# First attention of a two-block transformer kernel: statistics of later chunks taken earlier, right sums placed behind the key and value closes, and first roots by two tiles

## The chip, the cores and the metric

The kernel runs on one core of a Trainium2 chip. Its time is the device time of one execution in microseconds (us). Before the change, three executions took 1986.58, 1987.5 and 1990.99 us; the median is 1987.5. The engines are called as in the profile: PE is TensorE, with PEld for its weight loads, DVE is VectorE, ACT is ScalarE, POOL is GpSimd, and SP issues most DMAs.

## The reference

The input x holds 2048 tokens of 512 float32 features; a second sequence of the same size, ctx, supplies keys and values. Four layers follow one another, each on a layernorm of x and each added to x: an attention, a feed-forward layer, a second attention, and a mixture of experts. The change is in the first attention alone:

```python
q = (layernorm(x) @ Wq + bq).reshape(B, L, 8, 4, 128)         # 8 groups of 4 heads
k_, v_ = jnp.split(ctx @ Wkv + bkv, 2, axis=-1)               # 8 key and value heads
attn = softmax(einsum('bkglm,bmkd', scores of q and k) / sqrt(128))
x = x + (einsum('bkglm,bmkd->blkgd', attn, v).reshape(B, L, 4096) @ Wo + bo)
```

Attention runs within a sequence of 64 tokens (there are 32 of them). The layernorm of x needs a mean, a variance and an inverse square root for each token.

## The kernel before, in words

**Tiles and chunks.** The rows of x stay on the chip as 16 tiles of 128 tokens (`xs`); four tiles make a chunk of 512 tokens, and there are four chunks. The first attention is a loop over 32 turns, `order`: chunks 0 and 1 alternate through the eight groups of heads (turns 0 to 15), then chunks 2 and 3 do (turns 16 to 31). A turn computes one group's queries, scores and softmax for one chunk, and finishes the turn before it: turning the attention weights (`pt_o`), mixing the values (`po_o`) and projecting out to x (`ppx_o`, `ppy_o`, `ppz_o`).

**Products by seven quarters.** The large products (queries, keys and values, output) are made from seven products of quarter matrices instead of eight. This needs sums and differences of quarters on both sides: `left_sums` (L436 to L439) and `right_sums` (L446 to L449), four `tensor_tensor` instructions each. The weights' and context's sums run on POOL; those of the queries' right side, made from the normalised rows, run on DVE. A product is finished by a close, a DVE addition of a PSUM bank and a kept part: L641 for queries, L573 for keys and values. A PSUM bank can be used again only when its close has read it. The pool `ps_mm` has four banks and serves `pt_a`, `pz`, `py`, `pw`, `pt_o`, `pqy`, `pqz`, `pqv`, `po_o`, `ppy_o` and `ppz_o` in turn.

**The rows of a chunk.** Before a chunk's first turn, `attn0_in(c)` prepares its rows: `chunk_stats` takes mean and variance of each of the four tiles (L383, L386) and the inverse root of all four at once. Chunks 0 and 1 use `first_inv_sqrt` (two ACT steps, L368 and L369, then one Newton step), chunks 2 and 3 use `inv_sqrt` (three Newton steps on DVE, L353 to L362). DVE then writes a normalised tile h (L496), PE transposes it in four pieces (`pt_a`, L502), ACT copies it out of PSUM into `rows_q` (L507), and DVE makes the right sums. Chunk 1 is prepared after turn 0, chunk 2 after turn 15, chunk 3 after turn 16. At the end of each turn but the last few, `make_kv` makes keys or values for a later turn; it comes in the code after `attn0_in`. For chunks 2 and 3, `add_bias` adds the output bias to the rows of x on POOL (L486) once the rows h have been read.

**What sets the order.** A planner orders the instructions of each engine by its own costs. `pin` keeps an instruction in program order against other pinned ones of its engine. All of PE's matmuls in this stage are pinned; on DVE the query closes are pinned, and the statistics of chunks 2 and 3 (L383); on POOL the sums before turn 1 are pinned through the class `InOrder`. [...]

Of the kernel before, what the change touches and what calls it, by code (L numbers as in the profile page):

```python
# [12 lines left out]
ALU = mybir.AluOpType  # L13
# [9 lines left out]
TT = CH // P  # L23
# [6 lines left out]
def layers(ctx: ExitStack, tc: tile.TileContext, a: dict, out: bass.AP):  # L30
    nc = tc.nc
# [67 lines left out]
    def pin(ins):  # L99
        return tc.keep_in_program_order(ins)  # L100
# [92 lines left out]
    xs = [X[:, i, :] for i in range(NC * TT)]  # L193
# [218 lines left out]
    def chunk_stats(c, name, **how):  # L412
        return row_stats(xs[c * TT : (c + 1) * TT], name, **how)
# [28 lines left out]
    def right_sums(engine, b11, b12, b21, b22, sums, t3=None):  # L442

        t1, t2, t4 = (sums[:, i] for i in range(3))
        t3 = b12 if t3 is None else t3
        engine.tensor_tensor(t1, b12, b11, ALU.subtract)  # L446
        engine.tensor_tensor(t2, b22, t1, ALU.subtract)
        engine.tensor_tensor(t3, b22, b12, ALU.subtract)
        engine.tensor_tensor(t4, b21, t2, ALU.subtract)  # L449
        return {"11": b11, "21": b21, "22": b22, "1": t1, "2": t2, "3": t3, "4": t4}  # L450
# [25 lines left out]
    class InOrder:  # L476


        def tensor_tensor(self, *operands):
            pin(nc.gpsimd.tensor_tensor(*operands))  # L480

    adder = [InOrder()]

    def add_bias(c):
        for x in xs[c * TT : (c + 1) * TT]:
            adder[0].tensor_tensor(x, x, bo, ALU.add)  # L486

    def attn0_in(c):

        hx = rows_q[c % 2]  # L490
        roots = first_inv_sqrt, inv_sqrt
        mv, rstd = chunk_stats(c, f"a{c}", root=roots[c // 2], pinned=c > 1)
        for t in range(TT):
            x = xs[c * TT + t]
            h = t2(f"h_a{c}_{t}")
            nc.vector.tensor_scalar(  # L496
                h, x, mv[:, t, 0:1], rstd[:, t : t + 1], ALU.subtract, ALU.mult
            )
            pt = ps_mm(f"pt_a{c}_{t}")
            for k in range(KT):  # L500
                pin(
                    nc.tensor.transpose(  # L502
                        pt[:, k * P : (k + 1) * P], h[:, k * P : (k + 1) * P], ident
                    )
                )

            nc.scalar.copy(  # L507
                hx[:, t // 2 : t // 2 + 3 : 2, :, (t % 2) * P : (t % 2) * P + P],
                pt.rearrange("p (i k n) -> p i k n", i=2, k=2),
            )  # L510
        return right_sums(nc.vector, hx[:, 0], hx[:, 1], hx[:, 2], hx[:, 3], hx[:, 4:7])

# [20 lines left out]
    def ctx_right(c):  # L535
        x = ctx_q[c % 2]
        return right_sums(adder[0], x[:, 0], x[:, 1], x[:, 2], x[:, 3], ctx_sums[c % 2])

    def attn0_kv(value, g, c, left, right):
        n = f"{'kv'[value]}{g}_{c}"  # L540
        for i in range(2):
            kv[value, g + i, c] = kv_free.pop(0)
        dst = [kv_tiles[:, kv[value, g + i, c], :] for i in range(2)]

        def product(ps, x, y, first=True):
            x, y = left[x], right[y]
            for m in range(2 if value else 1):
                for k in range(2):
                    sides = (y[:, k, m * P : (m + 1) * P], x[:, k, :]) if value else (
                        x[:, k, :], y[:, k, :]  # L550
                    )
                    out_ps = ps[:, m * P : (m + 1) * P] if value else ps[:, 0:256]
                    pin(
                        nc.tensor.matmul(  # L554
                            out_ps, *sides, start=first and m == k == 0, stop=k == 1,
                            skip_group_check=True,
                        )
                    )

        kept = [t2(f"u_{n}_{i}") for i in range(2)]  # L560

        def keep(ps, i, at):
            u = kept[at // 2][:, at % 2 * 256 : at % 2 * 256 + 256]
            if value:
                nc.scalar.copy(u, ps[:, 0:256])
            else:
                nc.scalar.activation(
                    u, ps[:, 0:256], AF.Identity, bias=bkv[:, g + i : g + i + 1]
                )
            return u  # L570

        def close(i, half, ps, u):
            nc.vector.tensor_tensor(  # L573
                dst[i][:, half * 256 : half * 256 + 256], ps[:, 0:256], u, ALU.add
            )

        x = ps_tr(f"px_{n}")
        product(x, "11", "11")
        u1 = keep(x, 0, 0)
        z = ps_mm(f"pz_{n}")  # L580
        product(z, "1", "1")
        z1 = keep(z, 1, 1)
        y = ps_mm(f"py_{n}")
        product(y, "12", "21")
        close(0, 0, y, u1)
        product(x, "2", "2", first=False)
        u2 = keep(x, 0, 2)
        product(z, "4", "22", first=False)
        close(0, 1, z, u2)
        y = ps_mm(f"pw_{n}")  # L590
        product(y, "22", "4")
        product(x, "3", "3", first=False)
        u3 = keep(x, 1, 3)
        close(1, 1, x, z1)
        close(1, 0, y, u3)

# [161 lines left out]
    order = [(2 * i + j, g) for i in range(NC // 2) for g in range(NG) for j in range(2)]  # L758
# [8 lines left out]
    def kv_chunk(p, j):  # L767

        return 2 * (2 * p // NG) + j, 2 * p % NG

    def make_kv(value, p, j):
        c, g = kv_chunk(p, j)
        attn0_kv(value, g, c, kv_lefts[value], ctx_rights[c])

    rights = {0: attn0_in(0)}
    attn0_first_keys(0, 0, w_k)
    open_visit(0)
    kv_lefts = [kv_left(w_k, 0), None]
# [7 lines left out]
    for i in range(len(order) + 1):  # L786
        q = iter(())
        if i < len(order):
            c, g = order[i]
            visit = visits[i // 2]  # L790
            q = attn0_queries(g, c, visit["q"], rights[c])
        if last is not None:
            gl, cl, atl = last
            atT = attn0_turn(gl, cl, atl)
        next(q, None), next(q, None)
        if last is not None:
            o = attn0_out(gl, cl, attn0_mix(gl, cl, atT), visits[(i - 1) // 2]["o"])
        else:
            o = iter(())
        for _ in range(3):  # L800
            next(q, None)
        for _ in range(2):
            next(o, None)
            qT = next(q, None)
        next(o, None), next(o, None)
        if i < len(order):
            at = attn0_scores(g, c, qT)
            last = (g, c, at)
        else:
            fold_latent(latent)  # L810
        for _ in range(3):
            next(o, None)
        if i == len(order):
            break
        if i % 2 == 0:
            if i > 0:
                visit["o"] = right_sums(nc.gpsimd, *w_quarters(visit["w"][1]), wo_sums)
            if i // 2 + 1 < len(visits):
                w_next = load_attn0(order[i + 2][1], (i // 2 + 1) % 2)
        else:  # L820
            if i // 2 + 1 < len(visits):
                open_visit(i // 2 + 1)
            else:
                nc.sync.dma_start(gamma, a["gamma"].broadcast_to([P, HID]))
                nc.sync.dma_start(beta, a["beta"].broadcast_to([P, HID]))
                up, latent = load_up()
                ups = []
                for j in range(2):
                    k11, k12, k21, k22 = w_quarters(up[:, :, j * 512 : (j + 1) * 512])
                    ups.append(left_sums(nc.gpsimd, k11, k21, k12, k22, up_sums[j]))  # L830
            if i % 4 == 1:
                clear_list(i // 4)
        if i + 1 < len(order):
            cn, gn = order[i + 1]
            if cn not in rights:
                rights[cn] = attn0_in(cn)
                if cn > 1:
                    add_bias(cn)

        p, step = divmod(i, 4)  # L840
        if i == 0:
            add_bias(1)
            adder[0] = nc.gpsimd
            make_kv(0, 0, 1)
        if step < 2:
            make_kv(1, p, step)
        elif p + 1 < NP:
            make_kv(0, p + 1, step - 2)
        cp, gp = kv_chunk(p, step % 2)
        if step < 2 and gp == NG - 2 and cp + 2 < NC:  # L850
            load_ctx(cp + 2, ctx_q[cp % 2])
            ctx_rights[cp + 2] = ctx_right(cp + 2)
        if step == 0 and p + 1 < NP:
            kv_lefts[0] = kv_left(load_kv(kv_chunk(p + 1, 0)[1], 0), 0)
        elif step == 1 and p + 1 < NP:
            kv_lefts[1] = kv_left(load_kv(kv_chunk(p + 1, 0)[1], 1), 1)
# [164 lines left out]
    for c in range(NC):  # L1021
# [6 lines left out]
        else:  # L1028
            load_ctx(2, ctxT[2])
            mv, rstd = chunk_stats(0, "b0", rms=True)  # L1030
# [537 lines left out]
    for i in range(NI + 1):  # L1568
        c, b = divmod(i, 8)
# [161 lines left out]
```

## Time and profile before

| | |
|---|---|
| median of the runs | 1987.5 us |
| profiled execution | 1988.88 us |
| its span, first to last instruction | 1987.0 us |
| mean granted PE clock | 0.982 |
| PE, DVE, ACT, POOL busy | 95%, 53%, 26%, 28% of the span |
| first attention | from the start to about 1220 us |

A busy share is an average over the whole kernel; what a stage costs is read from that stage. Three views matter here. The windows view gives the busy time of each engine in a stretch, with the clock that the throttle granted to PE (1.00 is full speed). The chain of work that ended last, in order of time, names at each step the piece of work that set the end; where an engine other than PE stands in it, PE was waiting for that work. The timeline gives single instructions, and in brackets how long an engine was idle before one and what ended this.

### The profile page before, as it was taken

How to read it: one execution, taken by the hardware profiler on the slowest of the kernel's cores; microseconds unless marked ns; L12 is line 12 of the kernel's file. 1: busy time of each engine (PE TensorE's matmuls, PEld its weight loads, DVE VectorE, ACT ScalarE, POOL GpSimd, SP SyncE). 2: the span in 40 equal slices, each digit the busy share in tenths (PEclk: the TensorE clock that was granted, in tenths of full speed). 3: DMA queues.
4: the chain of work that ended last, by engine and by line, in shares of the span. 5: the costliest groups of instructions: out<-in, count | busy, mean ns of one | idle time of the engine just before them, and what ended most of it. 6: DMA issues, size and time to landing. Idle time of an engine off the chain costs nothing.

```text
span 1987.0 us, 26632 instructions
## 1 busy us (share of the span) xinstructions
PE 1888.4 (95%) x10544; PEld 1545.4 (78%) x10544; DVE 1056.9 (53%) x2077; ACT 519.9 (26%) x1019; POOL 548.3 (28%) x581
## 2 busy tenths in 40 slices
PE   7999999999998799999999999999999999879993
PEld 5888988889887698998998987787777776655441
DVE  6455445445546754454454456455466466663415
ACT  2211212212212222122122122311221565543221
POOL 7221121121322211211211211141344535540115
PEclk9999999999999899999999999999999999989997
DMA  9992110111210101111110012000004201214628
GB/s 330 307 301 89 39 43 33 33 43 40 67 43 11 43 33 32 43 32 33 43 32 22 22 59 88 19 1 11 0 22 138 64 12 54 85 71 133 217 94 271
DMA packets 129882, 151.72 MB, mean 76 GB/s; under 512 B 4704, under 2 KB 84384, under 8 KB 129760
## 3 DMA queue, kind: packets, MB, share of 16 engines
q1 hardware_dynamic: 118752, 122.70, 19.5%
q0 software_dynamic: 5392, 17.11, 2.6%
q10 hardware_dynamic: 5616, 10.23, 1.4%
q8 instruction: 84, 1.38, 0.3%
q14 instruction: 38, 0.31, 0.1%
HBM read 92.60 MB, written 56.36 MB: 75 GB/s over the span
## 4 chain that ended last, share of the span: by engine, by line
PE 88%; DVE 6%; DMA 2%; ACT 2%; issue 1%; POOL 1%; POOLq 0%; SPq 0%; DVEq 0%; ACTq 0%
PE ppx_o L464 11%; PE pqx_a L464 9%; PE sc_a L106 6%; PE pqz_a L464 6%; PE ppz_o L464 6%; PE py L106 6%; PE po_o L106 3%; PE pp L106 3%; PE pdx_f L464 3%; PE pqv_a L464 3%; PE ppy_o L464 3%; PE pqy_a L464 3%; PE px_v L554 2%; PE phx_f L464 2%; PE px_k L554 2%; PE pq_b L106 2%
## 5 line engine op out<-in xcount | busy, mean ns | idle before, releaser
L405 ACT ACTIVATE at_a<-at_a 128x512 f32<-128x512 f32 x64 | 40.4, 631 | 444.0 <-DVE at_a L404 444.0
L106 PE MATMUL py<-arena,xT 128*128 x312 | 140.8, 593 | 0.4 <-ACT xT L1447 0.2
L633 ACT ACTIVATE u_a<-pqx_a,bq 128x256 f32<-128x256 f32 x192 | 80.6, 471 | 163.4 <-PE pqx_a L464 161.1
L464 PE MATMUL ppx_o<-weights,oT_o 128*128 128x256 f32 x512 | 122.8, 383 | 0.1
L464 PE MATMUL pqz_a<-arena 128*128 128x256 f32 x512 | 121.0, 379 | 0.0
L464 PE MATMUL pqx_a<-arena,weights 128*128 128x256 f32 x512 | 121.0, 379 | 0.0
L106 PEld LDWEIGHTS sc_a<-kv,qT_a 128*128 128x128 f32 x1024 | 119.4, 192 | 1.7
L106 PE MATMUL sc_a<-kv,qT_a 128*128 128x64 f32 x1024 | 117.9, 273 | 0.0
L729 DVE TENSOR_TENSOR x<-ppx_o,x 128x512 f32<-128x512 f32 x128 | 86.9, 679 | 46.5 <-PE ppx_o L464 44.6
L464 PEld LDWEIGHTS pqz_a<-arena 128*128 128x128 f32 x512 | 97.2, 190 | 13.6 <-issue 0.4
L641 DVE TENSOR_TENSOR qT_a<-pqz_a,u_a 128x512 f32<-128x512 f32 x64 | 44.3, 692 | 113.9 <-ACT u_a L633 81.1
L464 PEld LDWEIGHTS pqx_a<-arena,weights 128*128 128x128 f32 x512 | 94.9, 190 | 12.0 <-DMA arena<-in_ctxT 0.2
L464 PEld LDWEIGHTS ppx_o<-weights,oT_o 128*128 128x128 f32 x512 | 94.8, 190 | 12.0 <-ACT oT_o L719 0.5
L106 PEld LDWEIGHTS py<-arena,xT 128*128 128x128 f32 x312 | 56.1, 190 | 56.5 <-issue 56.0
L446 POOL TENSOR_TENSOR arena<-weights 128x512 f32<-128x512 f32 x15 | 19.1, 1272 | 270.3 <-PE ppz_o L464 270.3
L436 POOL TENSOR_TENSOR arena<-weights 128x512 f32<-128x512 f32 x17 | 21.8, 1286 | 204.0 <-PE pqz_a L464 200.9
L436 POOL TENSOR_TENSOR kv_room<-weights 128x256 f32<-128x256 f32 x14 | 10.7, 762 | 238.6 <-DMA weights<-in_Wkv 238.6
L641 DVE TENSOR_TENSOR qT_a<-pqy_a,u_a 128x512 f32<-128x512 f32 x32 | 22.1, 692 | 101.5 <-PE pqy_a L464 101.5
L1466 DVE TENSOR_TENSOR y<-py,weights 128x512 f32<-128x512 f32 x39 | 26.9, 691 | 85.0 <-PE py L106 77.2
L403 DVE TENSOR_REDUCE mx_a<-sc_a 128x8 f32<-128x512 f32 x64 | 44.3, 692 | 44.3 <-PE sc_a L106 44.3
L106 PE MATMUL po_o<-atT_o,kv 64*128 64x256 f32 x512 | 65.9, 392 | 0.8 <-ACT atT_o L698 0.8
L1015 POOL TENSOR_TENSOR s_f<-s_f,arena 128x512 f32<-128x512 f32 x16 | 21.5, 1361 | 157.0 <-DVE s_f L1012 117.1
(427 smaller groups left out, 4264.9 us busy)
## 6 DMA issues: line engine op xcount, KB each, us to landing
xg<-zero SPq DMA_DIRECT2D x8, 4096.0 KB, 20.1
weights<-in_Wq SPq DMA_DIRECT2D x16, 1024.0 KB, 5.3
weights<-in_Wo SPq DMA_DIRECT2D x16, 1024.0 KB, 5.3
xr<-xg SPq DMA_DIRECT2D x39, 256.0 KB, 3.5
yg<-y ACTq DMA_DIRECT2D x39, 256.0 KB, 2.2
weights<-in_Wkv SPq DMA_DIRECT2D x16, 512.0 KB, 3.4
arena<-in_W_e SPq DMA_DIRECT2D x8, 1024.0 KB, 6.1
x<-in_x SPq DMA_DIRECT2D x16, 256.0 KB, 8.3
```

What stands on the lines that cost most here:

```text
L106: nc.tensor.matmul(ps, lhsT, rhs, start=(i == 0), stop=(i == len(pairs) - 1))
L403: nc.vector.tensor_reduce(mx, p3, AX.X, ALU.max)
L405: nc.scalar.activation(dst, dst, AF.Exp, scale=scale)
L436: engine.tensor_tensor(s1, a21, a22, ALU.add)
L446: engine.tensor_tensor(t1, b12, b11, ALU.subtract)
L464: nc.tensor.matmul(ps[:, m, :], left[:, k, m * P : (m + 1) * P], right[:, k, :], start=first and m == i == k == 0, stop=i == len(pairs) - ...
L554: nc.tensor.matmul(out_ps, *sides, start=first and m == k == 0, stop=k == 1, skip_group_check=True,)
L633: nc.scalar.activation(u[:, m * 256 : (m + 1) * 256], ps[:, m * 256 : (m + 1) * 256], AF.Identity, bias=bq[:, 4 * g + 2 * heads + m : 4 * ...
L641: nc.vector.tensor_tensor(q5[:, heads, :, 4 * half : 4 * half + 4, :], ps.rearrange("p (m b q) -> p m b q", m=2, q=64), u.rearrange("p (m ...
L729: nc.vector.tensor_tensor(dst, ps.rearrange("p (m n) -> p m n", m=2), dst, ALU.add)
L1015: nc.gpsimd.tensor_tensor(y, y, gamma, ALU.mult)
L1466: pin(nc.vector.tensor_tensor(y, py, be1[:, bass.ds(v[1], 1), :], ALU.add))
```

## The change

There are three parts. Each is in the first attention, and none changes what is computed.

The statistics and roots of chunks 2 and 3 are taken after turns 4 and 8, between that turn's output and its value product, and kept until the chunk's rows are made. The rows themselves are still asked for after turns 15 and 16.

`attn0_in` now returns the transposed rows only. Their right sums are a function of their own, `attn0_right`; for chunks 1, 2 and 3 it is called behind `make_kv`, and both its sums and the closes of keys and values are pinned in program order on DVE.

Chunks 0 and 1 take their roots by two tiles at a time instead of by four, still with `first_inv_sqrt`.

```diff
     class InOrder:
+        def __init__(self, engine):
+            self.engine = engine
+
         def tensor_tensor(self, *operands):
-            pin(nc.gpsimd.tensor_tensor(*operands))
-
-    adder = [InOrder()]
+            pin(self.engine.tensor_tensor(*operands))
+
+    adder = [InOrder(nc.gpsimd)]
...
-    def attn0_in(c):
+    def attn0_in(c, stats=None):
         hx = rows_q[c % 2]
-        roots = first_inv_sqrt, inv_sqrt
-        mv, rstd = chunk_stats(c, f"a{c}", root=roots[c // 2], pinned=c > 1)
+        if stats is None:
+            stats = []
+            for i in range(0, TT, 2):
+                mv, rstd = row_stats(
+                    xs[c * TT + i : c * TT + i + 2], f"a{c}_{i}", root=first_inv_sqrt
+                )
+                stats += [(mv[:, j, 0:1], rstd[:, j : j + 1]) for j in range(2)]
+        else:
+            mv, rstd = stats
+            stats = [(mv[:, j, 0:1], rstd[:, j : j + 1]) for j in range(TT)]
         for t in range(TT):
             x = xs[c * TT + t]
             h = t2(f"h_a{c}_{t}")
-            nc.vector.tensor_scalar(
-                h, x, mv[:, t, 0:1], rstd[:, t : t + 1], ALU.subtract, ALU.mult
-            )
+            nc.vector.tensor_scalar(h, x, *stats[t], ALU.subtract, ALU.mult)
...
-        return right_sums(nc.vector, hx[:, 0], hx[:, 1], hx[:, 2], hx[:, 3], hx[:, 4:7])
+        return hx
+
+    def attn0_right(hx, engine):
+        return right_sums(engine, hx[:, 0], hx[:, 1], hx[:, 2], hx[:, 3], hx[:, 4:7])
...
+    ordered = InOrder(nc.vector)
...
         def close(i, half, ps, u):
-            nc.vector.tensor_tensor(
+            ordered.tensor_tensor(
                 dst[i][:, half * 256 : half * 256 + 256], ps[:, 0:256], u, ALU.add
             )
...
-    rights = {0: attn0_in(0)}
+    rights, stats = {0: attn0_right(attn0_in(0), nc.vector)}, {}
...
             cn, gn = order[i + 1]
+            if i in (4, 8):
+                stats[i // 4 + 1] = chunk_stats(i // 4 + 1, f"a{i // 4 + 1}", pinned=True)
             if cn not in rights:
-                rights[cn] = attn0_in(cn)
+                hx = attn0_in(cn, stats.get(cn))
                 if cn > 1:
                     add_bias(cn)
...
             make_kv(0, p + 1, step - 2)
+        if i + 1 < len(order) and cn not in rights:
+            rights[cn] = attn0_right(hx, ordered)
```

## The prediction

> **What bounds the kernel now.** First the page's busy line and its chain by engine:
>
> ```profile
> PE 1888.4 (95%) x10544; PEld 1545.4 (78%) x10544; DVE 1056.9 (53%) x2077; ACT 519.9 (26%) x1019; POOL 548.3 (28%) x581
> ...
> PE 88%; DVE 6%; DMA 2%; ACT 2%; issue 1%; POOL 1%; POOLq 0%; SPq 0%; DVEq 0%; ACTq 0%
> ```
>
> TensorE carries the chain; VectorE is busy half the time, so its work costs only where TensorE waits for it. The windows view (span; then busy time and count of PE, PEld, DVE, ACT, POOL; granted clock, DMA share, GB/s) says where that is in the first attention:
>
> ```profile
> 78.00:560.00 482.00, 482.00 (x2760) 430.94 (x2760) 245.16 (x405) 102.55 (x208) 95.78 (x86) 1.00 0.28 85
> ...
> 604.00:624.00 20.00, 13.59 (x63) 11.75 (x64) 13.12 (x32) 5.54 (x11) 5.54 (x4) 0.83 0.08 27
> ...
> 656.00:678.00 22.00, 15.47 (x104) 14.07 (x105) 18.29 (x66) 5.75 (x12) 5.56 (x4) 0.77 0.00 1
> 678.00:1200.00 522.00, 522.00 (x2967) 465.73 (x2964) 266.23 (x440) 111.83 (x226) 95.66 (x84) 1.00 0.11 35
> ```
>
> Two stretches have no pause at all. Between them lie two pauses, one after turn 15 and one after turn 16, where the granted clock falls too. The chain (start, duration, what) says what TensorE waits for there, and shows two more places, at 10 and at 50 us:
>
> ```profile
> 7.43 0.70 DVE st_a L383
> ...
> 9.65 0.56 DVE h_a L496
> ...
> 48.39 1.67 DVE arena L449
> 50.06 0.34 DVE kv L573
> ...
> 603.29 0.69 DVE x L729
> 603.98 0.61 DVE st_a L383
> ...
> 609.40 3.83 DVE h_a L496 x4
> 613.37 1.08 PE pt_a L502 x4
> ```
>
> Each is VectorE preparing query rows: statistics (L383), root, normalised rows (L496), or the right sums (L446 to L449) ahead of the key and value closes (L573).
>
> **The two pauses.** I price them by turn length, which takes in the slow matmuls after a pause:
>
> ```profile
> 557.65 3.52 PE sc_a L106 x32
> 594.50 3.52 PE sc_a L106 x32
> ...
> 643.10 3.52 PE sc_a L106 x32
> 694.96 3.52 PE sc_a L106 x32
> 732.02 3.52 PE sc_a L106 x32
> ```
>
> From scores to scores a turn with a key product takes 36.85 (557.65 to 594.50), one with a value product 37.06 (694.96 to 732.02). The two in question take 48.60 and 51.86. Each must keep its 16 transposes: 16 times 0.109 us, from eight pt_o transposes in 0.87, makes 1.74. Without a pause they would take 38.59 and 38.80: gains of 10.0 and 13.1.
>
> Are the pauses really free of cover? In the built order of the changed program the statistics of chunks 2 and 3 leave this place for turns 4 and 8, and VectorE issues the four rows h_a inside turns 15 and 16: two behind the left sums, one behind the close of pqv, one behind the last query close. There VectorE idled 2.77 us (before L641 at 585.05) and 1.04 twice. A row costs 0.48 (1.92 for four, alone) to 1.3 (2.60 for two beside POOL): the first two need 2.6 at most and fit; the others may be 0.3 late, on closes that TensorE needs about 3 us later (pqv closes at 587.63; scores start at 594.34). So nothing; with that cover gone, 1.9 to 5.2 us a turn. The transposes then need four PSUM banks; the last is freed by the ppz add that ends at 602.40, before TensorE arrives at 603.27. The first attention's clean case is turn 0, where pt_a follows the scores at once and the key product follows 1.59 us later, never waiting for ACT's four 0.59 us copies.
>
> What slides into the emptied place is the FFN's statistics of chunks 0 and 1: four of L383 and their roots, 20 instructions, now before and between the first closes. Laid out from 602.5 with 0.6 us per statistic and 0.2 per dependent small step, the first close comes at about 607.9 (TensorE's py_k ends 607.7) and the second at 609.8. The first to wait for that second close is pt_o's second bank, at 603.27 + 1.74 + 6.06 (seven products of 0.866) + 0.44 = 611.5. Covered by 1.7 us. The four right sums, pinned behind the last close, take 2.7 (four L446 to L449 from 669.91 to 672.53) in a hole of 3.24 (idle before L641 at 677.35). Zero, with 0.5 to spare; the next in VectorE's queue is the query close of pqy, and po_o's second pair of banks waits for it. The bias adds on POOL (L486, 5.5 us) move ahead with the rows; in turn 15 three stand before L439, where POOL idled 4.86, and that sum isn't read for 20 us. SP's order and its DMAs don't change.
>
> **Turns 4 and 8.** Their statistics and roots (20 instructions, 603.90 to 609.36 in the trace, 5.46 us) are pinned between the last output add and the first value close. In turn 4 that add ends at 197.45, so the first close starts at 202.85 in place of 199.51, and the second, 0.34 behind it with 0.42 to run, ends at 203.62. The second pt_o bank waits for that, and was due at 203.25: 0.4 us lost, twice, -0.8. Ends: 0, and 2.5 if POOL slows every small step (one L361 took 1.23 beside POOL at 665.26); POOL has only L449 there, and L383 ran at its usual 0.69 beside POOL at 17.52, so I take 0.8.
>
> **The start.** The fourth tile's statistics start when its DMA lands, at 7.43, before and after. Then came mean, variance, two ACT steps, three Newton steps: first row at 9.65. By two tiles, the first pair's variance and ACT steps (0.2 each) run while VectorE waits for tiles three and four; three Newton steps of 0.2 are left behind 8.14, so the first row comes at 8.74. The second pair's steps slip between rows, and TensorE needs 0.91 per tile (3.65 for four), more than VectorE. Gain 0.9; the ceiling is the context. Its last DMA is issued around 5.2, lands 9.0 later at 14.2, and pk's third slice would now come at 14.6. I take 0.85; ends 0 and 0.95.
>
> **Turn 0's end.** Now the right sums of chunk 1 no longer stand before the closes. The second softmax product can start at 42.5 and, at 1.75 beside POOL, ends at 44.3; the closes follow, the second ends about 45.1, and TensorE's py_v starts at 46.71, behind pz_v, not at 50.45: 3.74 gained. But the sums still have to be made, from about 52.6 on, while POOL is still busy: its order is unbroken, and I put its 1.3 us adds until about 54 and its 0.73 us kv sums until 57. These rows show the price:
>
> ```profile
> 43.40 1.64 DVE L447 TENSOR_TENSOR arena<-arena 128x512 f32<-128x512 f32 x1
> ...
> 669.91 0.68 DVE L446 TENSOR_TENSOR arena<-arena 128x512 f32<-128x512 f32 x1
> ```
>
> 1.64 beside POOL, 0.68 alone. [...] By the row, where starts lie 1.67 apart (46.64, 48.31), 6.7. The query close of pqy behind them is due at 55.87 with 0.2 of reserve before po_o's second pair waits for its bank. [...] Row: 59.3, 3.2 lost, gain 0.5. But the later POOL operations are half as wide: one sum at 1.67 and three at about 1.2 (0.6 plus 0.6) end at 57.9, 1.8 lost, gain 1.9; without contention 3.7. I take 2.2, between the last two and nearer the contended one.
>
> **Sum:** 0.85 + 2.2 + 10.0 + 13.1 - 0.8 = 25.35. The profiled span is 1987.0 (its execution 1988.88, so 1.9 lies around the span) and becomes 1961.7; the median of the runs shown is 1987.5, so I predict 1962.1. All that follows is TensorE-paced and moves forward whole.
>
> **Rivals.** *A wait takes the place of the one removed.* The closes behind the newly placed statistics come later than laid out, and pt_o or po_o waits for its bank in turns 4, 8, 15 and 16. For it: VectorE's order is fixed, small steps can be blocked to 1.23, margins are 0.5 to 1.7. Against: POOL is idle at these places. With 2 to 3 us in each of four places the gain falls by about 10: some 1972.
>
> *The clock becomes the bound (slower).* The pauses are TensorE's only rest between 78 and 1200 us. If running on without them made the throttle grant less, everything would stretch: it eats 25.3 us over some 1,120 when the clock falls to 0.978, and at 0.95 the kernel ends at about 2020. Against: 482 and 522 us without a pause were granted 1.00.
>
> *The wait moves to another releaser and nothing is won.* The transposes could still have been held by PSUM or ACT behind VectorE, giving 1985 to 1989. Against: turn 0, and the built order leaves only one VectorE wait in them, the ppz add.
>
> **How the numbers follow.** Forecast 0.80, first rival 0.12, clock 0.03, nothing won 0.02, and 0.03 for a gain above 29 or a loss by what I haven't seen. The cost ends (start 0 to 0.95, turn 0 -0.6 to 3.7, pauses 21 to 23.3, turns 4 and 8 -2.5 to 0) give gains of 18 to 28; with half a us of run spread, 1958 to 1969; the first rival lies beyond. A measurement of this kernel tells 0.2% (4 us) from no change. Faster 0.95 (forecast, first rival), same 0.02, slower 0.03.
>
> **What would show it.** The transposes of turns 15 and 16 follow the output products without idle time, clock 1.00, scores to scores 38.6 and 38.8; first pt_a near 9.4; py_v near 45.8 (0.9 earlier, by the start) in turn 0, and then idle time of 1 to 2 us before po_o; 0.4 us before pt_o in turns 4 and 8. I am wrong if idle time at pt_o or po_o in turns 15 to 17 exceeds 1 us, or if the granted clock between 78 and 1200 is below 0.99.

## The result, and the profile after

The changed kernel takes 1961.95 us (median of four executions, 1961.05 to 1963.11), the kernel before 1987.04 beside it (1986.57 to 1990.99): 25.1 us less. The ratio is 0.9868 (95% interval 0.9854 to 0.9881); like every ratio below it is an estimate from all executions beside one another, not the quotient of the two medians, which is 0.9874 here. The forecast was 1962.1. The profiled execution took 1963.11, with a span of 1961.4 where the one before had 1987.0, so the spans differ by 25.6.

First the page's busy line and its chain by engine, of the changed kernel:

```profile
PE 1883.8 (96%) x10544; PEld 1542.4 (79%) x10544; DVE 1052.9 (54%) x2087; ACT 520.2 (27%) x1023; POOL 546.9 (28%) x581
...
PE 90%; DVE 5%; DMA 2%; ACT 1%; issue 1%; POOL 1%; POOLq 0%; SPq 0%; DVEq 0%; ACTq 0%
```

The matmuls are the same 10544. VectorE's share of the chain fell from 6% to 5% and TensorE's rose from 88% to 90%. VectorE's own busy time hardly moved (1056.9 to 1052.9): what went is TensorE's waiting, not VectorE's work. The windows of the changed kernel (span; busy time and count of PE, PEld, DVE, ACT, POOL; granted clock, DMA share, GB/s) put that in its place:

```profile
58.00:60.00 2.00, 2.00 (x12) 1.51 (x9) 1.33 (x3) 0.69 (x1) 0.27 (x1) 1.00 0.99 291
60.00:62.00 2.00, 2.00 (x11) 1.77 (x10) 1.97 (x4) 0.84 (x2) 0.00 (x0) 1.00 0.98 291
...
604.00:624.00 20.00, 20.00 (x104) 17.26 (x103) 13.18 (x32) 6.35 (x13) 5.65 (x6) 1.00 0.09 27
656.00:678.00 22.00, 22.00 (x120) 19.80 (x119) 12.41 (x21) 2.43 (x5) 5.03 (x4) 1.00 0.15 48
78.00:1175.00 1097.00, 1097.00 (x6249) 979.47 (x6249) 583.34 (x1016) 239.06 (x484) 217.76 (x192) 1.00 0.19 58
```

The stretches from 604 and from 656 us had 13.59 of 20 and 15.47 of 22 us of TensorE work, at a clock of 0.83 and 0.77. Now both are full at 1.00, and so is the whole stretch from 78 to 1175 us. The first two rows are for the experiments below. The chain of the changed kernel (start, duration, what):

```profile
7.61 0.69 DVE st_a L383
...
8.93 0.45 DVE h_a L508
...
9.52 3.51 PE pt_a L512 x16
...
45.89 0.89 PE py_v L570 x8
...
54.69 1.11 PE po_o L106 x8
55.80 1.20 DVE arena L483
57.00 0.61 DVE qT_a L657
57.61 0.04 issue
57.65 1.13 PE po_o L106 x6
58.78 1.92 PE pqx_a L464 x8
...
598.90 1.73 PE ppx_o L464 x8
600.63 1.75 PE pt_a L512 x16
602.37 0.87 PE px_k L570 x4
```

In turn 15 the 16 transposes start the moment the output product ends (598.90 + 1.73) and the key product follows at once. In turn 0, py_v starts without a wait, and further on po_o stops half way: the chain runs over a right sum (it stands under the line of the helper that pins it, L483) and the query close L657, and po_o resumes at 57.65.

From scores to scores, from the chain:

| stretch | before | after | predicted |
|---|---|---|---|
| start to scores of turn 0 | 33.61 | 32.63 | 32.76 |
| turn 0 | 43.62 | 41.89 | 41.42 |
| turns 4 and 8, each | 37.05 | 37.08, 37.09 | 37.45 |
| turn 15 | 48.60 | 38.60 | 38.59 |
| turn 16 | 51.86 | 38.79 | 38.80 |

### The profile page after: what moved, and what is told of

Its sections match the earlier page's. It is cut to its first block, busy times and chain, and to the rows that moved or that the text cites. A ratio compares the mean times of both kernels' runs of the same rounds, so it can differ in the third digit from the quotient of the medians.

```text
span 1961.4 us, 26634 instructions
## 1 busy us (share of the span) xinstructions
PE 1883.8 (96%) x10544; PEld 1542.4 (79%) x10544; DVE 1052.9 (54%) x2087; ACT 520.2 (27%) x1023; POOL 546.9 (28%) x581
## 4 chain that ended last, share of the span: by engine, by line
PE 90%; DVE 5%; DMA 2%; ACT 1%; issue 1%; POOL 1%; POOLq 0%; SPq 0%; DVEq 0%; ACTq 0%
PE ppx_o L464 11%; PE pqx_a L464 9%; PE py L106 6%; PE sc_a L106 6%; PE pqz_a L464 6%; PE ppz_o L464 6%; PE po_o L106 3%; PE pp L106 3%; PE pdx_f L464 3%; PE pqy_a L464 3%; PE ppy_o L464 3%; PE pqv_a L464 3%; PE px_v L570 2%; PE phx_f L464 2%; PE px_k L570 2%; PE pq_b L106 2%
## 5 line engine op out<-in xcount | busy, mean ns | idle before, releaser
L405 ACT ACTIVATE at_a<-at_a 128x512 f32<-128x512 f32 x64 | 40.4, 631 | 444.0 <-DVE at_a L404 444.0
L657 DVE TENSOR_TENSOR qT_a<-pqz_a,u_a 128x512 f32<-128x512 f32 x64 | 44.3, 692 | 112.0 <-ACT u_a L649 79.5
L657 DVE TENSOR_TENSOR qT_a<-pqy_a,u_a 128x512 f32<-128x512 f32 x32 | 22.1, 691 | 91.2 <-PE pqy_a L464 91.2
```

Source lines behind the costliest of these rows:

```text
L405: nc.scalar.activation(dst, dst, AF.Exp, scale=scale)
L657: nc.vector.tensor_tensor(q5[:, heads, :, 4 * half : 4 * half + 4, :], ps.rearrange("p (m b q) -> p m b q", m=2, q=64), u.rearrange("p (m ...
```

## The experiments

Nothing of the computation is left out in any of these kernels. They ran in three series of four, each on its own chip, beside which the kernel before took 1994.04, 1990.26 and 1988.79 us. So I compare ratios to it, turn lengths within one profile, and medians within one series. My theory is the prediction's: two pauses removed are worth 23.1 us and don't depend on the small parts; the small parts are worth what VectorE's order and POOL beside it allow. The rivals are given with each run.

**Roots by four again.**

```diff
-            for i in range(0, TT, 2):
+            for i in range(0, TT, 4):
...
-                    xs[c * TT + i : c * TT + i + 2], f"a{c}_{i}", root=first_inv_sqrt
+                    xs[c * TT + i : c * TT + i + 4], f"a{c}_{i}", root=first_inv_sqrt
```

> The changed kernel with the first chunks' roots by four tiles again; all else as changed. My theory (the first pair's steps run while the last tiles land): the first transpose comes at 10.3 again instead of 9.5, turn 0's scores at 33.6 instead of 32.6, all turn lengths as in the changed kernel, 1.0 us slower: about 1963.0. Rival (the earlier start is eaten further on, by context or POOL): turn 0's scores stay at 32.6 to 33.0 and the time within 0.3 of 1962.

1968.64 us, ratio 0.9864 (0.9848 to 0.9880). Its median says nothing of one microsecond; its profile does. From the fourth tile's statistics to the first row it took 2.10 us (7.14 to 9.24), in the kernel before 2.22 (7.43 to 9.65), in the changed one 1.22 (7.61 to 8.83). So roots by two tiles are worth 0.9 to 1.0 us, counted from the start of the fourth tile's statistics. The starts I had named did not come: the first transposes began at 9.94 and turn 0's scores at 33.00, the upper edge of the rival's range, because in this execution the fourth tile's statistics began 0.29 earlier than in the kernel before, and the key product was 0.2 shorter. And turn 0 took 43.52 us and not 41.89, with the same right sums, query close and `po_o` as in the changed kernel. I come back to that.

**Right sums ahead of the closes again.**

```diff
-                hx = attn0_in(cn, stats.get(cn))
+                rights[cn] = attn0_right(attn0_in(cn, stats.get(cn)), ordered)
...
-        if i + 1 < len(order) and cn not in rights:
-            rights[cn] = attn0_right(hx, ordered)
```

> The changed kernel with the right sums of chunks 1 to 3 pinned ahead of the key and value closes. My theory: turn 0 goes back from 41.9 to about 43.6, because TensorE waits for the key closes; turns 15 and 16 stay at 38.6 and 38.8, because there the sums can start 3.1 us after the transposes do, take 2.7, and the second close still beats pt_o's second bank; 1.7 us slower, about 1963.7. Rival (the order of sums and closes is part of what emptied the pauses): turns 15 and 16 grow by 2 us or more each, 1968 or above.

1970.38 us, ratio 0.9873 (0.9856 to 0.9889). Turns 15 and 16 were 38.59 and 38.80: the order of sums and closes is not what frees them. Turn 0 took 44.66; py_v waited 3.0 us, and then eight matmuls took 1.73 in place of the 1.16 of the kernel before: the clock had fallen (0.50 from 52 to 54 us).

**Statistics of chunks 2 and 3 back behind turns 15 and 16.**

```diff
-            if i in (4, 8):
-                stats[i // 4 + 1] = chunk_stats(i // 4 + 1, f"a{i // 4 + 1}", pinned=True)
+            if i in (15, 16):
+                stats[i - 13] = chunk_stats(i - 13, f"a{i - 13}", pinned=True)
```

> The changed kernel with the statistics of chunks 2 and 3 taken after turns 15 and 16 again. My theory: the pauses come back whole, turns of about 48.6 and 51.9, 23 us slower, about 1985. Rival (moving the sums behind the closes did a good part of it): turns of 43 to 46, 1974 to 1980.

1990.49 us, ratio 0.9981 (0.9973 to 0.9989). The pauses are back: 47.77 and 51.45 us. The chain of this variant in turn 15:

```profile
606.70 3.84 DVE h_a L508 x4
610.54 0.14 issue
610.67 0.81 PE pt_a L512 x4
```

The rows come 6.1 us after TensorE's last output product (598.83 + 1.74 = 600.57), behind four statistics and their roots. This variant keeps both small parts and gains 0.19% (3.6 us by the medians); in its profile 1.2 us of its gain are shorter pauses.

**Early statistics, late rows.** The statistics stay behind turns 4 and 8; the four rows of chunks 2 and 3 are pinned behind the last softmax step of turns 15 and 16.

```diff
-        nc.vector.tensor_tensor(d3, d3, rs[:, :, None].broadcast_to([P, 8, 64]), ALU.mult)
+        last_op = nc.vector.tensor_tensor(
+            d3, d3, rs[:, :, None].broadcast_to([P, 8, 64]), ALU.mult
+        )
+        if name in ("a7_1_1", "a0_2_1"):
+            pin(last_op)
...
-            nc.vector.tensor_scalar(h, x, *stats[t], ALU.subtract, ALU.mult)
+            row = nc.vector.tensor_scalar(h, x, *stats[t], ALU.subtract, ALU.mult)
+            if c > 1:
+                pin(row)
```

> The changed kernel with the early statistics kept, but the normalised rows of chunks 2 and 3 pinned behind the last softmax step of turns 15 and 16, so that they come behind the last output add. It separates the statistics from the rows, which the planner moved by itself. My theory: the rows start 0.65 us after the output products end and take 3.8 beside POOL's bias adds, so the last tile's transposes start 4.6 us after the output products in place of 1.3: turns of about 41.9 and 42.1, 6.6 us slower, about 1968.5. If the rows cost nothing there (statistics are all): 38.6 and 38.8, 1962.

1977.48 us, ratio 0.9908 (0.9891 to 0.9925); turns 15 and 16 took 42.42 and 42.98, 8.0 us more together where I had expected 6.6. The rows in a block (3.75 us from 604.53, transposes at 608.41) stand between softmax and transposes. So of the 23.1 us of both pauses, 8.0 come from rows that the planner may move into VectorE's holes once their statistics are there, and 15.1 from the statistics alone.

**Chunk 1's bias adds after turn 1**, so that POOL is free earlier beside the right sums.

```diff
         if i == 0:
+            make_kv(0, 0, 1)
+        if i == 1:
             add_bias(1)
+        if i == 2:
             adder[0] = nc.gpsimd
-            make_kv(0, 0, 1)
```

With it POOL's sums stay pinned (`adder`) for two turns longer.

> The changed kernel with chunk 1's bias adds on POOL moved from the end of turn 0 behind turn 1's query sums. My theory (the four right sums behind the closes are slow only because POOL reads the SBUF beside them): the sums take 2.7 us instead of 5.5, the query close is on time, po_o does not wait, turn 0 takes 40.4 instead of 41.9; 1.5 us faster than the changed kernel, about 1960.5. Rival (the place in the queue costs, whatever POOL does): turn 0 stays at 41.9, 1962.

1963.46 us, ratio 0.9868 (0.9845 to 0.9892). The four sums took 4.09 us in place of 5.53, not 2.7: POOL still made three half as wide sums (128x256) beside them. po_o's wait shrank to 0.04, but turn 0 came to 41.30, not 40.4. Its chain says why:

```profile
39.17 5.50 DVE at_a L410
...
46.74 1.16 PE py_v L570 x8
```

The multiply of the first of turn 0's two softmaxes, 0.82 us long in the changed kernel, took 5.50 here, beside POOL's bias adds; the second softmax, the closes and py_v came late (py_v waited 0.6). Those adds are chunk 0's, which this edit does not move, so the slow multiply can't be put down to the edit. The four right sums took 5.53 us in the changed kernel and 4.09 here, beside POOL's work, and 2.61 in the changed kernel's turn 15 with POOL idle; what in POOL's work makes them longer isn't shown.

**Right sums on POOL**, ahead of chunk 1's bias adds.

```diff
         if i == 0:
+            rights[1] = attn0_right(hx, adder[0])
             add_bias(1)
```

> The changed kernel with the right sums of chunk 1 made on POOL, ahead of its bias adds. Both theories of the wait at po_o expect the same here, that it goes: turn 0 at 40.4. It tells whether POOL is early enough: its four sums should end near 54 and the second query product needs them near 56.5. If POOL is late, TensorE waits there instead and turn 0 stays near 41.9 or above. About 1960.5 if it holds.

1961.3 us, ratio 0.9861 (0.9838 to 0.9885). Turn 0 took 39.78 us, 2.1 less than in the changed kernel's profile and 0.6 better than I expected: with the sums off VectorE, po_o doesn't wait at all. Its chain there, to be read against the one of the changed kernel:

```profile
55.44 1.98 PE po_o L106 x16
```

So the wait of 1.48 us cost the changed kernel more than its length: po_o took 4.09 us from its first matmul to its last (54.69 to 58.78) in place of 1.98, which is the whole difference of 2.1.

**Both chunks' statistics behind turn 4.**

```diff
-            if i in (4, 8):
-                stats[i // 4 + 1] = chunk_stats(i // 4 + 1, f"a{i // 4 + 1}", pinned=True)
+            if i == 4:
+                for k in (2, 3):
+                    stats[k] = chunk_stats(k, f"a{k}", pinned=True)
```

> The changed kernel with both chunks' statistics after turn 4: twice the VectorE work in front of one turn's value closes. My theory (the second bank of pt_o waits for the second close): closes from 205.4, that bank 5.5 us late, turn 4 at 42.5 and turn 8 back at 37.05; 5.4 us slower, about 1967.4. Rival (that bank waits for nothing here, the first to wait is po_o at 204.6): turn 4 at 38 to 39, 1963 to 1964.

1966.2 us, ratio 0.9884 (0.9859 to 0.9910). Turn 4 took 39.10, only 2.05 more than 37.05, so the second close isn't what pt_o needs. The timeline of this variant there (start, duration, engine, line, operation, tiles; idle time before it and releaser in brackets):

```profile
203.44 0.60 PE L712 MATMUL pt_o<-ident,at_a 128*128 128x128 f32 x4
204.72 0.66 PE L712 MATMUL pt_o<-ident,at_a 128*128 128x128 f32 x4 [0.68 <-ACT atT_o L714]
...
208.76 0.42 DVE L483 TENSOR_TENSOR kv<-py_v,u_v 128x256 f32<-128x256 f32 x1
209.10 0.41 DVE L483 TENSOR_TENSOR kv<-pz_v,u_v 128x256 f32<-128x256 f32 x1
209.24 2.72 PE L106 MATMUL po_o<-atT_o,kv 64*128 64x256 f32 x16 [0.41 <-DVE kv L483]
```

The second half of pt_o runs at 204.72, more than 4 us ahead of both closes: it lost 0.68, and the profile names ACT's copy of the first half. The first instruction that waits for a close is po_o, 0.41 us for the first of them; its 16 matmuls then took 2.72 in place of 2.05 in the kernel before. That is the rival's reading, though turn 4 lies 0.1 above its range.

**Bias adds later and chunk 1's roots by four.**

```diff
-            for i in range(0, TT, 2):
+            w = 4 if c else 2
+            for i in range(0, TT, w):
...
         if i == 0:
+            make_kv(0, 0, 1)
+        if i == 1:
             add_bias(1)
+        if i == 2:
             adder[0] = nc.gpsimd
-            make_kv(0, 0, 1)
```

> The kernel with chunk 1's bias adds behind turn 1, and with chunk 1's roots by four tiles again (chunk 0's by two). My theory: ACT's second pair of root steps for chunk 1 delays the key eviction and the first query bias, and TensorE's second product waits 0.14 us and runs late by 0.25 for it; without them turn 0's scores come 0.2 earlier, at 32.4, and the rest is as with the bias adds moved: about 1960.3. Rival: the 0.14 has another cause (POOL) and nothing changes, 1960.5.

1962.68 us, ratio 0.9871 (0.9850 to 0.9893); turn 0 was 40.05, and the second query product started without the 0.14 us wait that it has in the changed kernel. That doesn't show the cause: the variant with the bias adds moved and roots by two had no such wait either (its product started 3.45 us after the first, as here). In none of the six profiles with chunk 1's roots by four does the product come late, and in five of the eight with roots by two it does, in two of them for POOL. That ACT's second pair of root steps has a part in it is likely and not shown. The multiply that had taken 5.50 us didn't hold up the second softmax here: its sums over the rows began at 39.86 in place of 44.59, with the bias adds in the same place.

**What does the wait at po_o cost?** In the variants with roots by four, late rows or both statistics at turn 4, turn 0 took 43.52, 43.60 and 43.58 us; in the changed kernel and with late statistics, 41.89 and 41.85. All five have the same right sums, query close and po_o in turn 0. The windows showed the clock near half behind po_o's wait in the first three. So I ran the changed kernel again, unedited:

> The changed kernel itself once more, nothing edited. In it the output product po_o of turn 0 waits 1.5 us for the query close behind the four right sums. Theory: what that wait costs is not fixed; in some executions TensorE's granted clock falls to about 0.56 for some 3.4 us after it, and turn 0 then takes 43.5 us instead of 41.9. So this execution shows either 41.9 with clock 1.00 from 58 to 64 us, or 43.5 with a clock of 0.5 to 0.7 in two microseconds of that stretch. Rival: the 43.5 us turns of the earlier variants belong to their edits (order of roots, of rows, of statistics), and this kernel always shows 41.9. Turns 15 and 16 are 38.6 and 38.8 by both; ratio to the kernel before 0.986 to 0.988.

1964.71 us (1960.57 to 1965.18), ratio 0.9870 (0.9853 to 0.9886). Its windows, to be read against the first two rows of the changed kernel's above:

```profile
58.00:60.00 2.00, 1.43 (x6) 0.97 (x6) 1.18 (x2) 0.38 (x1) 1.19 (x2) 0.71 1.02 302
60.00:62.00 2.00, 2.00 (x5) 1.38 (x5) 1.44 (x2) 0.31 (x1) 0.00 (x0) 0.50 1.01 297
62.00:64.00 2.00, 2.00 (x10) 1.70 (x10) 1.90 (x4) 0.64 (x2) 0.00 (x0) 0.94 0.99 292
```

And its chain:

```profile
58.58 1.84 PE po_o L106 x6
60.42 2.85 PE pqx_a L464 x8
```

Turn 0 took 43.51. In 2 us, five matmuls instead of eleven, at a clock of 0.50: po_o's six took 1.84 in place of 1.13 and pqx_a's eight 2.85 in place of 1.92, together 1.64 more. The theory holds; the slow turns didn't belong to the edits. The table has every profile with a wait of TensorE in turn 0 beyond 0.1 us:

| execution | wait of TensorE, us | clock behind it | turn 0 |
|---|---|---|---|
| changed | 1.48, po_o | 1.00 | 41.89 |
| late statistics | 1.44, po_o | 1.00 | 41.85 |
| roots by four | 1.46, po_o | 0.56, 0.59 | 43.52 |
| changed, again | 1.46, po_o | 0.71, 0.50 | 43.51 |
| late rows | 1.51, po_o | 0.50, 0.65 | 43.60 |
| both at turn 4 | 1.53, po_o | 0.57, 0.58 | 43.58 |
| bias adds later | 0.6, py_v | 1.00 | 41.30 |
| sums ahead of closes | 3.0, py_v | 0.50, 0.66 | 44.66 |
| early statistics alone (below) | 3.1, py_v | 1.00 | 43.16 |
| before | 3.6, py_v | 1.00 | 43.62 |

(Wait: the idle time before the product that is named. Clock: of the one or two windows of 2 us behind the wait.) The wait's length doesn't decide: 1.46 cost the clock, and 3.1 and 3.6 didn't. In each of the five falls, behind waits of 1.46 to 3.0 us, the windows together lack 1.7 us of full clock. With the 0.50 of the lowest windows I estimate from that 3.4 us at half clock. What decides whether a wait is followed by a fall isn't shown by any run here.

**Sums on POOL and roots by four for chunk 1, and sums on POOL alone,** in one series with the changed kernel.

> Chunk 1's right sums on POOL ahead of its bias adds, and chunk 1's first roots by four tiles, chunk 0's by two as in the changed kernel. Theory: with the sums off VectorE po_o no longer waits in turn 0, so no clock can fall there: turn 0 takes 39.8 to 39.9 us and the second query product starts without its 0.14 us wait; turns 15 and 16 stay 38.6 and 38.8. That is 2.0 us and more below the changed kernel of the same call: ratio to it 0.9985 or less. Rival: the eight more microseconds of POOL work ahead of the bias adds make the left sums, rows or copies late, and what is won at po_o is lost by py_v or by the key product of turn 1: turn 0 of 41.5 us or more and no difference in time.

> The right sums on POOL alone, chunk 1's roots by two tiles, again, for its interval beside the changed kernel. Theory: turn 0 of 39.8 us, the time 1.5 to 3.5 us below the changed kernel. Rival: within 0.5 us of it. Against the variant with roots by four for chunk 1 no difference beyond 0.3 us is expected.

Turn 0 took 39.78 and 39.77 us, clock 1.00 behind po_o in both: no wait, no fall. The times are 1961.92 (1961.52 to 1964.79) and 1962.42 (1960.37 to 1965.11) beside 1964.71: 2.8 and 2.3 us less by the medians, which is near the size expected (the quotient of the first is 0.9986, where I had said 0.9985 or less; the two differ by 0.5 where I had said 0.3), but the ranges overlap, so that either beats the changed kernel isn't shown by the times. The second had its scores of turn 0 only at 35.59, because a context transfer took 9.96 us:

```profile
3.72 9.96 DMA arena<-in_ctxT
13.68 0.14 issue
13.81 9.43 PE pk L106 x16
```

Over all fourteen profiles the scores of turn 0 start between 32.5 and 35.6 us. In the three latest (34.28, 35.27, 35.59) the chain begins with one transfer of context or query weights of 9.96 to 11.69 us. That spread is more than any of the small parts is worth.

**Early statistics alone**: roots by four, and sums ahead of the closes, as in the two edits above.

> Only the early statistics of chunks 2 and 3 are left of the change: the right sums stand ahead of the closes and the first roots are by four tiles, as before. Theory: the parts add up. Turns 15 and 16 take 38.6 and 38.8, turn 0 43.6 to 44.7 and its scores start as before, so the gain is 23.1 less 0.1 for turns 4 and 8 and the half microsecond lost behind the attention: ratio to the kernel before 0.9880 to 0.9890. Rival: the parts depend on each other (with the sums ahead of the closes TensorE is later in turn 0 and the later stages move), so the gain is under 20 us: ratio above 0.9900.

1964.88 us (1963.57 to 1966.18), ratio 0.9876 (0.9859 to 0.9892), span 1964.4: turns 15 and 16 at 38.59 and 38.80, turn 0 at 43.16. This part alone carries the change: the ratio is just below the range expected, and in this series the time equals the changed kernel's (1964.71). In the two profiles the changed kernel's scores of turn 1 started at 77.08 us (33.57 + 43.51), this one's at 76.97 (33.81 + 43.16): with the clock fallen in the one and not in the other, the two small parts brought nothing there. In the profiles of the two kernels themselves they brought 77.23 - 74.52 = 2.7.

## Why the prediction was right, and where it wasn't

**The two pauses** (10.0 + 13.1) came as worked out: 38.60 and 38.79, clock 1.00. No rival took hold: the profile lists no wait of TensorE between 78 and 1190 us. Chunk 1's and 0's FFN statistics in the emptied place, the four rows, and the right sums cost TensorE nothing. The step that let the rows go free, the holes in VectorE's order within turns 15 and 16, is confirmed by the variant with late rows, where that cover is gone: 3.8 and 4.2 us a turn, inside the 1.9 to 5.2 given.

**The clock as bound** is out: 1,097 us from 78 to 1175 without a pause, granted 1.00.

**The start** (0.85): 0.98 in the profile. Roots by two tiles gave 0.9 to 1.0, as laid out, and the context was no ceiling in that execution. The first transposes came 0.82 earlier, with the last tile 0.18 later. pt_a and pk ran 0.55 shorter, and 0.38 was lost at the second query product; neither was in the forecast, and that they nearly offset is luck. What I left out is how much landings vary between executions.

**Turn 0's end** (2.2): 1.73 in the profiled execution, and near 0.1 (43.62 - 43.51) in four of the six profiles that have these instructions, with a fallen clock there and none in the kernel before. (With the sums ahead of the closes the clock can fall too: 44.66 with a fall and 43.16 without, in two variants.) The steps held: py_v at 45.89 without a wait, as forecast; and the sums took, in the timeline of the changed kernel,

```profile
51.14 0.42 DVE L483 TENSOR_TENSOR kv<-pw_v,u_v 128x256 f32<-128x256 f32 x1
51.47 5.53 DVE L483 TENSOR_TENSOR arena<-arena 128x512 f32<-128x512 f32 x4
56.92 0.68 DVE L657 TENSOR_TENSOR qT_a<-pqy_a,u_a 128x512 f32<-128x512 f32 x1
```

5.53 us for four where I had estimated 5.3 (1.67 and three at 1.2), and 2.61 in turn 15 with POOL idle. From 54.13 on POOL's operations were half as wide, as I had assumed, and took 1.05 to 1.18 until the sums ended. The -0.6 at the low end of the range for turn 0 is shown by no run; in its place they showed 1.73, and near 0.1 with the clock fallen. The step that failed is "1.8 lost": it prices a wait by its length. The idle time was 1.48; against the 39.78 of a turn without it, it cost 2.1 with the clock kept and 3.7 with the clock fallen.

**Turns 4 and 8** (-0.8): they lost 0.03 and 0.04. The step "the second pt_o bank waits for that" is wrong. In the timeline of the changed kernel's turn 4:

```profile
200.04 0.42 DVE L483 TENSOR_TENSOR kv<-py_v,u_v 128x256 f32<-128x256 f32 x1
200.10 1.07 PE L712 MATMUL pt_o<-ident,at_a 128*128 128x128 f32 x8
200.38 0.41 DVE L483 TENSOR_TENSOR kv<-pz_v,u_v 128x256 f32<-128x256 f32 x1
```

All eight transposes start at 200.10 and run through, while the second close still runs until 200.79. The variant with both statistics at turn 4 says what would wait: first pt_o's second half for ACT's copy (0.68 us), then po_o for the first close (0.41 us). I had named a bank's releaser from the order of allocation, and no wait in the trace before had shown it. The same wrong bank stood behind the 1.7 us of cover in turn 15; there nothing waited by either reading.

**The sum.** 25.35 was forecast for the span and 25.6 measured, but not term by term: +0.13 at the start, -0.47 in turn 0, -0.03 in the pauses, +0.73 in turns 4 and 8; one turn of 37.41 us in the profile before, which has no counterpart after, adds 0.36; and of 26.05 us ahead at the scores of the last turn, 0.45 were given back behind the attention. These offset one another: that the sum fits better than its terms is luck. The 37.41 is one `po_o` of 2.33 us in place of 1.98; two of the other profiles have one such turn each, elsewhere, and its cause is open. The 0.45 lies in the second attention: 16 matmuls behind a wait for POOL, which both kernels have, took 0.48 longer. The timeline of the kernel before, of the changed kernel, and of the changed kernel run again:

```profile
1795.63 5.41 PE L106 MATMUL pp<-weights,mix_last 128*128 128x256 f32 x16 [4.25 <-POOL mix_last L1175]
1769.61 5.89 PE L106 MATMUL pp<-weights,mix_last 128*128 128x256 f32 x16 [4.24 <-POOL mix_last L1195]
1771.80 5.41 PE L106 MATMUL pp<-weights,mix_last 128*128 128x256 f32 x16 [4.25 <-POOL mix_last L1195]
```

The clock was 0.61 and 0.53 in the two windows of 2 us from 1796 in the kernel before, and 0.50 in all three from 1768 in the changed one. Run again, the changed kernel took the 5.41 of the kernel before, so the loss belongs to that execution and not to the change.

## What to carry to other kernels

Small vector work for a later stage (statistics, roots) is best done many turns ahead, in any hole of its engine: that was 15 of the 23 us, and the other 8 came because rows with their statistics ready could be moved by the planner too. Price such a pause by whole turns, from one mark to the same mark of the next, which takes in the slow matmuls behind it (the stretches from 604 and 656 us had a granted clock of 0.83 and 0.77 with the pauses, 1.00 without). A short wait of TensorE should be given two prices, with the clock kept and with the half-clock stretch behind it (2.1 and 3.7 us for the 1.48 here), and the bank or tile that is said to wait should be one that a trace has shown waiting.

## What the runs showed that I had not expected

The same wait of about 1.5 us was followed by half clock in four of six executions, at 1.64 us more for the matmuls behind it, and waits of 3.1 and 3.6 us were not.

VectorE beside POOL isn't slowed by a fixed factor. The multiply at L410 took 0.82 us in the changed kernel, 1.80 in the kernel before, and 5.50 in the first variant with chunk 1's bias adds moved. There it outlasted four POOL adds in a row, as POOL's timeline of that variant shows:

```profile
37.97 4.93 POOL L483 TENSOR_TENSOR x<-x,bo 128x512 f32<-128x512 f32 x4
42.87 1.26 POOL L483 TENSOR_TENSOR arena<-weights 128x512 f32<-128x512 f32 x1
44.20 1.60 POOL L483 TENSOR_TENSOR arena<-weights,arena 128x512 f32<-128x512 f32 x1
```

It began at 39.17, inside the four adds (chunk 0's, which stand there in both kernels), and ended at 44.67. In the changed kernel the same four adds took 5.88 in place of 4.93, with VectorE's work going through between them. What decides whether VectorE gets in between is open.
